# A two-part kernel: the weights and the first image chunk of part two load into two tiles of part one

## The chip, the cores and the metric

The kernel runs on one core of a Trainium2 chip. TensorE (PE) multiplies matrices into PSUM, VectorE (DVE), ScalarE (ACT) and GpSimd (POOL) work on SBUF, and SyncE (SP) issues most of the DMAs; POOL issues the others. The metric is the time of one execution on the device in microseconds, as the median of several runs. One more execution is recorded by the hardware profiler; the profile and the trace are of that one.

## The reference

The input is x, 16 images of 64 channels of 128 x 128, float32. Two layers follow each other.

```
# layer 0: filtered nonlinearity
q = quantile(x over the pixels, 0.5)                # one median per image and channel
x = x + relu(-q)
y = upsample by 2, 7-tap filter along both axes; relu; 7-tap filter; every second pixel
# layer 1: frequency gate, then attention with reduced keys
spec = rfft2(y); gate = sigmoid(w2 gelu(w1 |spec|))
xf   = y + irfft2(spec * gate)
q    = xf as tokens @ q_w + q_b                     # 16384 tokens per image, 4 heads of 16
for (stride, weights) in ((8, sr1), (16, sr2)):     # 256 and 64 positions
    s = layernorm(conv(xf, weights, stride) + b); k, v = s @ kv_w + kv_b; v = depthwise 3x3 of v
out  = softmax(q k^T / 4) v @ proj_w + proj_b + y
```

## The kernel before

The work is done in two parts, `phase1` (line 262) and `phase2` (line 978). Each opens its own SBUF and PSUM pools, and closes them at its end; the second part's tiles lie where the first part's lay. Between them stand two sets of tensors in DRAM: `zd` (the filtered images y) and `xfd` (the gated images xf).

**The first part** goes over 16 images in groups of four channels, 256 groups in all. `filtered` (558) loads a group into one of four `pad` tiles, adds the image's shift on POOL (from a tile `sb`), and does the filters and the two steps of the transform. `gate` (727) and `inverse` (893) follow for each image, some groups later, and store `xfd`. The shifts come from `medians` (330), which takes two images at once: it loads them whole into two tiles, `xm` (302), 128 partitions by 8192 floats each, and finds the median of each of the 128 rows by counting on ACT and DVE. Its end is a chain over SP: `row<-mean` writes the 128 results to DRAM, and `sb<-row` (537) reads them back onto all partitions. POOL cannot shift the first group of a pair of images before `sb` is there. The last pair of images (14 and 15) is decided when some 30 groups are still to come; after that the tiles `xm` are used no more.

**The second part** goes over 256 periods, 16 for each image, of 1024 pixels. In a period it multiplies for the queries of one such stretch (`queries`, 1317, tokens Q), finds the row maxima of the scores of another (M), the exponents of a third (S and T), and the weighted values (V) and the projection (P) of a fourth. `fetch` (1285) loads the pixels (`xa`, by SP) and reorders them on POOL (`xo`). The maxima go from DVE through a small DMA, `carry` (1379, `q<-nt`), into the queries' tile, and the scores S wait for it. The result leaves on POOL's queue.

Keys and values are made by `keys_values` (1047) for two images at a time. It convolves four image chunks `c`, each 128 x 2 x 16 x 128 floats (2.1 MB), held in turn by two tiles `xp`, with the weights `s1` (stride 8) and `s2` (stride 16); each chunk is loaded in eight pieces from `xfd`. For the first two images this stands ahead of everything else (`spread` is false). For the later pairs its steps are spread over the periods of the pair before: `key` sets their place, and `gate_of` ties a load to the queries of a period.

```
key = (start + CONV[1] * c + k // 3) * 100 + 50 if spread else first + c      # line 1083
deps = [gate_of(start + CONV[1] * c + k // 3)] if spread else []
```

**What sets the order.** Both parts collect `Work` items and hand them to `planned` (158), a list scheduler with estimated durations. For each engine it looks at the first 60 items in order of their keys; items that can start now go by key, and when none of them can start soon, the one that can start first goes. In the second part PE keeps to the order of its keys alone. What the plan returns is issued through `put` (122), which holds each engine to that order. An engine does one thing after the other, so an item that must wait holds up what stands behind it; this includes the DMA issues on SP's and POOL's queues.

The loads of the second part's weights are not in a plan: they stand ahead of it.

```
nc.sync.dma_start(out=w2s, in_=w2)      # line 1019
nc.sync.dma_start(out=s1, in_=sr1)
nc.sync.dma_start(out=s2, in_=sr2)
for vb in vbs:
    nc.sync.dma_start(out=vb, in_=vinit)
```

One detail of `load` in `keys_values` (1075): it takes `y`, `i`, `h`, `c` and `xp` as they are when it is made, but `k` as it is when it runs. By then `k` holds the last value of a later loop, 4, so that for the first two images all 32 pieces are issued by SP, and none by POOL; the trace has them so (xp<-xfd on SP: 32).

Of the kernel before, what the change touches and what calls it, by code (L numbers as in the profile page):

```python
# [8 lines left out]
F32 = mybir.dt.float32  # L9
# [9 lines left out]
B, C, H, W = 16, 64, 128, 128  # L19
NPIX = H * W  # L20
HALF = NPIX // 2
# [45 lines left out]
W2_AT, W2_N = _cols(_W2)  # L67
# [36 lines left out]
@with_exitstack  # L104
def spectral_gate_attention(ctx: ExitStack, tc: tile.TileContext, x, cst, vinit, w1, w2, sr1, sr2, out):
    nc = tc.nc

    const = ctx.enter_context(tc.tile_pool(name="const", bufs=1))
    dram = ctx.enter_context(tc.tile_pool(name="dram", bufs=1, space=DRAM))
    csb = const.tile([128, CST_N], F32, name="csb")  # L110
    nc.sync.dma_start(out=csb, in_=cst)

    def cs(name, rows=128):
        return csb[0:rows, CST_AT[name]]

    ident = cs("ident")
    zd = [dram.tile([C, H, W], F32, name=f"zd{b}") for b in range(B)]
    xfd = [dram.tile([C, H, W], F32, name=f"xfd{b}") for b in range(B)]

    last = {}  # L120

    def put(op, *args, **kw):
        engine = op.__self__
        with tc.issue_after(last[engine]) if engine in last else nullcontext():
            out = op(*args, **kw)  # L125
        last[engine] = out.ins
        return out

    phase1(tc, nc, cs, ident, x, w1, dram, zd, xfd, put)
    phase2(tc, nc, cs, ident, vinit, w2, sr1, sr2, zd, xfd, out, put)  # L130


DELAY = {("PE", "ACT"): 267, ("PE", "DVE"): 210}
# [8 lines left out]
class Slot:  # L142


    def __init__(self, kind, fixed=None):
        self.kind, self.fixed, self.users, self.at = kind, fixed, [], None
# [112 lines left out]


@with_exitstack
def phase1(ctx, tc, nc, cs, ident, x, w1, dram, zd, xfd, put):

    G = 4
    NG = C // G
    P = 2 * G
    NP = NG // 2
    wp = ctx.enter_context(tc.tile_pool(name="p1w", bufs=1))
# [12 lines left out]
    sets, rooms = {}, {}  # L281
# [17 lines left out]
    room("pad", 4, G, W + 2 * PAD)  # L299
    room("bank", 2, 512, pool=psp)  # L300
    room("pair", 3, 2, 512, pool=psp)
    xm = [wp.tile([128, HALF], F32, name=f"xm{f}", tag=f"xm{f}") for f in range(2)]
    hit = wp.tile([128, 4096], U8, name="hit", tag="hit")
    hidl = wp.tile([16, 128], F32, name="hidl", tag="hidl")
    for t in sets["pad"]:
# [244 lines left out]
    over = []  # L550
    for b in range(0, B, 2):
        start = (b - 2) * NG
        over = medians(b, over, *((start, start + LAST) if b else (-99, -98)))
# [406 lines left out]
    for b in range(B):  # L960
        gate(b)
        for j in range(NP):
            inverse(b, j)

    for w in planned(works, rooms, AHEAD, STAY, SOON, REST):
        w.run()
# [7 lines left out]
CONV, CHAIN, TAPS = (2, 2), (14, 20, 23, 24, 28), 5  # L974


@with_exitstack
def phase2(ctx, tc, nc, cs, ident, vinit, w2, sr1, sr2, zd, xfd, out, put):

    N = 512  # L980
    NP = HALF // N
# [1 line left out]
    wp = ctx.enter_context(tc.tile_pool(name="p2w", bufs=1))  # L983
    psp = ctx.enter_context(tc.tile_pool(name="p2ps", bufs=1, space=PSUM))

    def tile_(name, *shape, pool=wp):
        return pool.tile(list(shape), F32, name=name, tag=name)

    w2s = tile_("w2s", 128, W2_N)
    s1 = tile_("s1", 128, 4, 8, C)  # L990
    s2 = tile_("s2", 128, 8, 16, C)
    vbs = [tile_(f"vb{i}", 128, 384) for i in range(4)]
    kgs = [tile_(f"kg{i}", 128, 2, NK) for i in range(2)]
    eps = tile_("eps", 128, 1)
    sets, rooms = {}, {}

    def room(kind, n, *shape, pool=wp):
        sets[kind] = [tile_(f"{kind}_{i}", 128, *shape, pool=pool) for i in range(n)]
        rooms[kind] = n
# [9 lines left out]
    room("nm", 4, 32)  # L1009
    room("nt", 4, 32)  # L1010
    room("rd", 2, N // 32)
    room("xp", 2, 2, 16, W)
    room("pair", 4, 2, 512, pool=psp)
    KVN = 2 * NK
    acc, xs, xc, sd = (tile_(n, 128, KVN) for n in ("acc", "xs", "xc", "sd"))
    pads = [tile_(f"vpad{size}", 64, 2, size + 2, size + 2) for size in (16, 8)]
    vt = tile_("vt", 64, 2, NK + NK2)

    nc.sync.dma_start(out=w2s, in_=w2)
    nc.sync.dma_start(out=s1, in_=sr1)  # L1020
    nc.sync.dma_start(out=s2, in_=sr2)
    for vb in vbs:
        nc.sync.dma_start(out=vb, in_=vinit)
    for t in sets["nm"] + pads:
        nc.gpsimd.memset(t, 0.0)
    nc.vector.memset(eps, 1e-5)
# [6 lines left out]
    def tile_of(slot):  # L1033
        return sets[slot.kind][slot.at]
# [3 lines left out]
    def work(engine, took, deps, key, run, every=None, shape=None, takes=(), tiles=range(8), back=False):  # L1038
        w = Work(engine, took, took if every is None else every, deps, key, run, shape, takes, tiles, back)
        works.append(w)  # L1040
        return w
# [3 lines left out]
    known, last_conv, held = {}, [[], []], {}  # L1045

    def keys_values(b, start, spread):
# [3 lines left out]
        first = start * 100  # L1051
        pair_of = {}

        def pe_key(period, k=0):
            return (start + period) * 100 + KV_AT + 0.01 * k if spread else first + period + 0.01 * k
# [9 lines left out]
            return work(engine, took, deps, key, run, back=spread, **kw)  # L1065

        part = {"A": (slice(0, 512), 0, 512), "B": (slice(512, 640), 1, 128)}
        sums = {"A": None, "B": None}
        for c in range(4):
            xp = Slot("xp", c % 2)  # L1070
            loads = []
            for k in range(8):
                y, i, h = k // 4, k // 2 % 2, k % 2

                def load(y=y, i=i, h=h, c=c, xp=xp):
                    src = xfd[b + i].rearrange("c (r d y) w -> y d c r w", y=2, d=4)[y, c]
                    queue = nc.gpsimd if spread or k % 2 else nc.sync
                    put(
                        queue.dma_start, out=tile_of(xp)[64 * y : 64 * y + 64, i, 8 * h : 8 * h + 8],
                        in_=src[:, 8 * h : 8 * h + 8],  # L1080
                    )

                key = (start + CONV[1] * c + k // 3) * 100 + 50 if spread else first + c
                deps = [gate_of(start + CONV[1] * c + k // 3)] if spread else []
                engine = "POOL" if spread or k % 2 else "SP"
                loads.append(
                    work(engine, 3500, deps + loads[:1], key, load, 700 if engine == "POOL" else 60, takes=[] if k else [xp])
                )
            for n, s in enumerate("AB"):
                cols, bank, m = part[s]  # L1090
                ps = Slot("pair", KV_SLOT)
                wgt = s1 if s == "A" else s2

                def convolve(s=s, ps=ps, xp=xp, c=c, bank=bank, m=m, wgt=wgt):
                    o = tile_of(ps)
                    if s == "A":
                        src = tile_of(xp).rearrange("p i a (h f e) -> p (i a) h f e", h=2, f=8)
                        taps = [(wgt[:, c, f, :], src[:, :, :, f, :]) for f in range(8)]
                    else:
                        src = tile_of(xp).rearrange("p i (a s) (f e) -> p (i a) s f e", s=2, f=16)  # L1100
                        taps = [(wgt[:, c + 4 * d, f, :], src[:, :, d, f, :]) for d in range(2) for f in range(16)]
                    for j, (w, x) in enumerate(taps):
                        put(
                            pe.matmul, o[64 * (j % 2) : 64 * (j % 2) + 64, bank, 0:m], w, x,
                            start=(j < 2), stop=(j >= len(taps) - 2),
                        )

                w = work(
                    "PE", 3430, loads, pe_key(CONV[0] + CONV[1] * c + n, n), convolve, shape="128x64", takes=[ps]
                )  # L1110
                xp.users.append(w)

                def add(s=s, ps=ps, c=c, cols=cols, bank=bank, m=m):
                    o = tile_of(ps)[:, bank, 0:m]
                    if c == 0:
                        put(v.tensor_scalar, acc[:, cols], o, wt("srb1" if s == "A" else "srb2", 128), None, ALU.add)
                    elif c < 3:
                        put(v.tensor_tensor, acc[:, cols], o, acc[:, cols], ALU.add)
                    else:
                        n = 2 if s == "A" else 1  # L1120
                        to = xs[:, cols].rearrange("p (a e h) -> p h a e", h=n, e=8)
                        o, a = (t.rearrange("p (a h e) -> p h a e", h=n, e=8) for t in (o, acc[:, cols]))
                        for h in range(n):
                            put(v.tensor_tensor, to[:, h], o[:, h], a[:, h], ALU.add)

                sums[s] = work(
                    "DVE", 760 if m > 128 else 360, [w] + ([sums[s]] if sums[s] else []),
                    pe_key(CONV[0] + CONV[1] * c + n, n) + 1, add,
                )
                ps.users.append(sums[s])  # L1130
# [11 lines left out]
        ps, w = product(CHAIN[0], 1070, list(sums.values()), center, "128x64")  # L1142
# [20 lines left out]
        ps, w = product(CHAIN[1], 1070, squares, spread_, "64x64")  # L1163
# [38 lines left out]
        ps, w = product(CHAIN[2], 1070, normed, keys, "64x128")  # L1202
# [71 lines left out]
    paces = {}  # L1274

    def gate_of(period):
        return paces[period]

    xas, xos, zrs, qs, qe, crossed, es, ex, avs, ons, vdone = {}, {}, {}, {}, {}, {}, {}, {}, {}, {}, {}

# [365 lines left out]
```

## Time and profile before

| | |
|---|---|
| runs | 9550.02 us median of 3 (9549.4 to 9576.27) |
| profiled execution | 9579.59 us, span 9577.8 us |
| mean granted TensorE clock | 0.969 |
| first part, end of its last matmul | 3930.8 us |
| last matmul of the first pair's convolutions | 4017.5 us |
| DMA queue of SP / of POOL | 423.45 MB / 125.88 MB |

All times within the execution count from the start of its span. In a row of the timeline stand the start, the duration, the engine, the line of the kernel, the operation with its output and input tile, and how many of them were merged; in brackets is the idle time of the engine before it and what ended it. Nearly all instructions carry line 125, since `put` issues them, so they are told apart by their tiles. A row of the waits names who waited, for whom, the sum in us, how often, and the longest. A row of the windows gives the length of the stretch, the busy time of PE, PEld, DVE, ACT and POOL with their counts, then the granted TensorE clock, the DMA share and GB/s.

### The profile page before, as it was taken

To read this page: it belongs to the slowest core of one execution; us is meant where nothing else is said; L and a number is where in the kernel's file an instruction comes from. 1 tells how busy PE (TensorE), PEld (TensorE's weight loads), DVE (VectorE), ACT (ScalarE), POOL (GpSimd) and SP (SyncE) were. 2 spreads that over 40 slices of the span, in tenths; PEclk is the share of its full clock that TensorE was granted. 3 is DMA by queue.
4 is the path that set the end of the run, shared out by engine and by line. 5 is a ranking of instruction groups with operands and counts; after the bars stand their busy time and mean duration, and the time that the engine had idled before them with its cause. 6 is when DMAs were issued, how large, how long until landed. Compare 5 with 4: busy or idle time off the path is not lost.

```text
span 9577.8 us, 176847 instructions
## 1 busy us (share of the span) xinstructions
PE 8901.4 (93%) x70144; PEld 4366.4 (46%) x70144; DVE 7588.5 (79%) x11754; ACT 5883.2 (61%) x7833; POOL 1338.7 (14%) x1390
## 2 busy tenths in 40 slices
PE   0798989898989999699999999999999999999999
PEld 0455555555555566344344344344344443444443
DVE  6797878787878787278878878878878778788887
ACT  2869697978787877245545545545555555455555
POOL 0121212121212121011111111111111111111110
PEclk9899999999999999799999999999999999999999
DMA  3132313131313122421121221221211211211111
GB/s 73 45 84 60 96 52 94 53 93 51 95 54 95 52 64 59 99 62 42 45 64 41 52 60 39 55 55 39 62 48 41 63 48 39 71 40 42 39 42 34
DMA packets 603626, 560.76 MB, mean 59 GB/s; under 512 B 86552, under 2 KB 497696, under 8 KB 594336
## 3 DMA queue, kind: packets, MB, share of 16 engines
q1 hardware_dynamic: 560288, 423.45, 16.8%
q0 software_dynamic: 42496, 125.88, 5.3%
q8 instruction: 554, 9.08, 0.4%
q14 instruction: 288, 2.36, 0.1%
HBM read 343.59 MB, written 201.33 MB: 57 GB/s over the span
## 4 chain that ended last, share of the span: by engine, by line
PE 50%; DVE 8%; issue 2%; DMA 2%; ACT 1%; SPq 1%; POOL 0%; ACTq 0%; POOLq 0%; DVEq 0%
PE pair L125 48%; DVE at L125 3%; DVE on L125 2%; DVE nm L125 2%; PE bank L125 2%; DMA q<-nt 1%; SPq L125 1%; DVE rd L125 0%; DMA xp<-xfd 0%; ACT e L125 0%; DVE sd L125 0%; POOL xo L125 0%; DVE vt L125 0%; ACT L125 0%; POOL pad L125 0%
## 5 line engine op out<-in xcount | busy, mean ns | idle before, releaser
L125 ACT ACTIVATE e<-pair 128x1024 f32<-128x1024 f32 x2560 | 2584.5, 1023 | 2566.8 <-PE pair L125 2556.8
L125 DVE TENSOR_REDUCE nm<-pair 128x2 f32<-128x640 f32 x4096 | 3208.6, 818 | 711.0 <-PE pair L125 672.0
L125 PE MATMUL pair<-kg,q 32*128 32x320 f32 x16384 | 2815.5, 468 | 43.9 <-DVE nm L125 41.7
L125 PE MATMUL pair<-q,kg 32*128 32x512 f32 (+1 forms) x12288 | 2644.1, 625 | 33.7 <-DMA q<-nt 28.8
L125 PEld LDWEIGHTS pair<-kg,q 32*128 32x128 f32 x16384 | 1254.7, 185 | 1590.8 <-DVE nm L125 1094.5
L125 DVE SCALAR_TENSOR_TENSOR z<-y,w1s,z 128x512 f32<-128x512 f32 x1536 | 1224.4, 801 | 345.9 <-ACT z L125 322.2
L125 PE MATMUL pair<-e,vb 128*32 128x512 f32 (+1 forms) x12288 | 1273.9, 603 | 0.9 <-DVE ot L125 0.9
L125 DVE SCALAR_TENSOR_TENSOR up<-pad,w1s,up 128x524 f32<-128x524 f32 x1280 | 1041.5, 841 | 181.4 <-ACT up L125 178.9
L125 PEld LDWEIGHTS pair<-q,kg 32*128 32x128 f32 (+1 forms) x12288 | 747.1, 165 | 609.9 <-DVE nm L125 209.2
L125 PE MATMUL pair<-up,w1s 64*128 64x262 f32 x4096 | 657.1, 430 | 312.0 <-DVE up L125 243.6
L125 POOL TENSOR_TENSOR pad<-pad,sb 128x512 f32<-128x512 f32 x256 | 454.9, 1782 | 2449.6 <-DMA pad<-x 1548.5
L125 ACT ACTIVATE r<-pair 128x524 f32<-128x524 f32 x1024 | 576.9, 615 | 153.5 <-PE pair L125 152.7
L125 POOL COPY xo<-xa 128x512 f32<-128x512 f32 x256 | 268.8, 1050 | 2745.2 <-issue 2500.8
L125 PEld LDWEIGHTS pair<-up,w1s 64*128 64x128 f32 x4096 | 400.3, 199 | 518.8 <-DVE up L125 239.6
L125 PE MATMUL pair<-r,w1s 128*64 128x262 f32 x4096 | 580.5, 408 | 44.3 <-ACT r L125 42.4
L125 PEld LDWEIGHTS pair<-e,vb 128*32 128x32 f32 (+1 forms) x12288 | 261.3, 108 | 668.1 <-issue 551.5
L125 POOL DMA_DIRECT2D result<-ot x512 | 272.5, 537 | 2081.9 <-DVE ot L125 2065.0
L125 PE MATMUL pair<-f,csb 128*128 128x260 f32 (+1 forms) x2048 | 521.8, 398 | 17.9 <-ACT f L125 16.4
L125 PE MATMUL bank<-csb,spec 128*64 128x256 f32 x4096 | 502.6, 390 | 15.0 <-ACT rc L125 10.6
L125 ACT ACTIVATE up<-pad,w1s 128x524 f32<-128x524 f32 x512 | 395.2, 805 | 153.3 <-POOL pad L125 153.3
L125 PEld LDWEIGHTS pair<-f,csb 128*128 128x128 f32 x2048 | 374.6, 193 | 157.0 <-issue 49.6
L125 PEld LDWEIGHTS pair<-r,w1s 128*64 128x64 f32 x4096 | 262.6, 140 | 281.6 <-ACT r L125 71.7
(150 smaller groups left out, 9162.3 us busy)
## 6 DMA issues: line engine op xcount, KB each, us to landing
xm<-x SPq DMA_DIRECT2D x128, 512.0 KB
pad<-x SPq DMA_DIRECT2D x256, 256.0 KB
zd<-z SPq DMA_DIRECT2D x256, 256.0 KB
xfd<-xf SPq DMA_DIRECT2D x256, 256.0 KB
xa<-xfd SPq DMA_DIRECT2D x512, 128.0 KB
zr<-zd SPq DMA_DIRECT2D x512, 128.0 KB
result<-ot POOLq DMA_DIRECT2D x512, 128.0 KB, 2.9
xp<-xfd POOLq DMA_DIRECT2D x224, 256.0 KB, 5.3
```

The costliest lines, as they stand in the source:

```text
L125: out = op(*args, **kw)
```

## The change

The two tiles `xm` move into a pool of their own, `kept`, that lasts over both parts. A class `Held` lays tiles of the second part into them: `s1`, `w2s`, the image chunk tile `xp` number 0 and three of the four `vb` into the first, `s2` into the second. `Held.loads` lists 22 loads: the weights `w2s`, three times `vinit`, `s1` in two pieces, `s2` in eight, and chunk 0 of the first two images in eight. The first part makes SP items of them, with keys from group 226 on and dependent on the last medians. The second part loads only the fourth `vb` itself, and for the first two images no chunk 0.

Further, all image loads of the later pairs get keys and gates three periods earlier; loads of chunks 2 and 3 of the first pair depend on the convolutions that free their tile; and `load` now takes `k` as it is when it is made, so that for the first pair every second piece is issued by POOL.

```
+    kept = ctx.enter_context(tc.tile_pool(name="kept", bufs=1))
+    xm = [kept.tile([128, HALF], F32, name=f"xm{f}", tag=f"xm{f}") for f in range(2)]
+    held = Held(xm)
+    phase1(tc, nc, cs, ident, x, w1, dram, zd, xfd, put, xm, held.loads(nc, vinit, w2, sr1, sr2, xfd))
+    phase2(tc, nc, cs, ident, vinit, zd, xfd, out, put, held)
...
+    def loads(self, nc, vinit, w2, sr1, sr2, xfd):
+        yield self.w2s, w2
+        for vb in self.vbs:
+            yield vb, vinit
+        for d in range(0, 4, 2):
+            yield self.s1[:, d : d + 2], sr1[:, d : d + 2]
+        for d in range(8):
+            yield self.s2[:, d], sr2[:, d]
+        for k in range(8):
+            yield image_chunk(self.xp, xfd, 0, 0, k)
...
@@ phase1
-    xm = [wp.tile([128, HALF], F32, name=f"xm{f}", tag=f"xm{f}") for f in range(2)]
...
+    for k, (o, i) in enumerate(late):
+        work("SP", 4000, over, B * NG - 30 + k, lambda o=o, i=i: put(nc.sync.dma_start, out=o, in_=i), 60)
...
@@ phase2
-    w2s = tile_("w2s", 128, W2_N)
-    s1 = tile_("s1", 128, 4, 8, C)
-    s2 = tile_("s2", 128, 8, 16, C)
-    vbs = [tile_(f"vb{i}", 128, 384) for i in range(4)]
+    w2s, s1, s2 = kept.w2s, kept.s1, kept.s2
+    vbs = kept.vbs + [tile_("vb3", 128, 384)]
...
-    room("xp", 2, 2, 16, W)
+    sets["xp"], rooms["xp"] = [kept.xp, tile_("xp1", 128, 2, 16, W)], 2
...
-    nc.sync.dma_start(out=w2s, in_=w2)
-    nc.sync.dma_start(out=s1, in_=sr1)
-    nc.sync.dma_start(out=s2, in_=sr2)
-    for vb in vbs:
-        nc.sync.dma_start(out=vb, in_=vinit)
+    nc.sync.dma_start(out=vbs[3], in_=vinit)
...
@@ keys_values
-            for k in range(8):
-                y, i, h = k // 4, k // 2 % 2, k % 2
-
-                def load(y=y, i=i, h=h, c=c, xp=xp):
+            for k in range(8) if spread or c else ():
+
+                def load(k=k, c=c, xp=xp):
...
-                key = (start + CONV[1] * c + k // 3) * 100 + 50 if spread else first + c
-                deps = [gate_of(start + CONV[1] * c + k // 3)] if spread else []
+                period = start + CONV[1] * c + k // 3 - 3
+                key = period * 100 + 50 if spread else first + c
+                deps = [gate_of(period)] if spread else convs[c - 2] if c > 1 else []
...
     def gate_of(period):
-        return paces[period]
+        return paces[max(0, period)]
```

More of the change, by code (lines that the diff above doesn't have):

```diff
@@ L127, in put, with __init__, image_chunk @@
         return out
-    phase1(tc, nc, cs, ident, x, w1, dram, zd, xfd, put)
-    phase2(tc, nc, cs, ident, vinit, w2, sr1, sr2, zd, xfd, out, put)
+    kept = ctx.enter_context(tc.tile_pool(name="kept", bufs=1))
[3 more added lines that the diff above has]
+    phase2(tc, nc, cs, ident, vinit, zd, xfd, out, put, held)
+class Held:
+    def __init__(self, xm):
+        ends = [0]
+        for n in (4 * 8 * C, W2_N, 2 * 16 * W, 384, 384, 384):
+            ends.append(ends[-1] + n)
+        s1, w2s, xp, *vbs = (xm[0][:, a:b] for a, b in zip(ends, ends[1:]))
+        self.s1, self.w2s, self.vbs = s1.rearrange("p (d f o) -> p d f o", d=4, f=8), w2s, vbs
+        self.xp = xp.rearrange("p (i r w) -> p i r w", i=2, r=16)
+        self.s2 = xm[1].rearrange("p (d f o) -> p d f o", d=8, f=16)
+    def loads(self, nc, vinit, w2, sr1, sr2, xfd):
[8 more added lines that the diff above has]
+            yield image_chunk(self.xp, xfd, 0, 0, k)
+def image_chunk(xp, xfd, b, c, k):
+    y, i, h = k // 4, k // 2 % 2, k % 2
+    rows = xfd[b + i].rearrange("c (r d y) w -> y d c r w", y=2, d=4)[y, c]
+    return xp[64 * y : 64 * y + 64, i, 8 * h : 8 * h + 8], rows[:, 8 * h : 8 * h + 8]
 DELAY = {("PE", "ACT"): 267, ("PE", "DVE"): 210}
@@ L261, in phase1 @@
 @with_exitstack
-def phase1(ctx, tc, nc, cs, ident, x, w1, dram, zd, xfd, put):
+def phase1(ctx, tc, nc, cs, ident, x, w1, dram, zd, xfd, put, xm, late):
     G = 4
@@ L977, in phase2 @@
 @with_exitstack
-def phase2(ctx, tc, nc, cs, ident, vinit, w2, sr1, sr2, zd, xfd, out, put):
+def phase2(ctx, tc, nc, cs, ident, vinit, zd, xfd, out, put, kept):
     N = 512
@@ L1067, in keys_values @@
         part = {"A": (slice(0, 512), 0, 512), "B": (slice(512, 640), 1, 128)}
-        sums = {"A": None, "B": None}
+        sums, convs = {"A": None, "B": None}, []
         for c in range(4):
@@ L1071, in keys_values @@
             loads = []
-            for k in range(8):
-                y, i, h = k // 4, k // 2 % 2, k % 2
-                def load(y=y, i=i, h=h, c=c, xp=xp):
-                    src = xfd[b + i].rearrange("c (r d y) w -> y d c r w", y=2, d=4)[y, c]
+            for k in range(8) if spread or c else ():
+                def load(k=k, c=c, xp=xp):
                     queue = nc.gpsimd if spread or k % 2 else nc.sync
[L1078 to L1081, printed above, removed]
-                key = (start + CONV[1] * c + k // 3) * 100 + 50 if spread else first + c
-                deps = [gate_of(start + CONV[1] * c + k // 3)] if spread else []
+                    o, i = image_chunk(tile_of(xp), xfd, b, c, k)
+                    put(queue.dma_start, out=o, in_=i)
+                period = start + CONV[1] * c + k // 3 - 3
+                key = period * 100 + 50 if spread else first + c
+                deps = [gate_of(period)] if spread else convs[c - 2] if c > 1 else []
                 engine = "POOL" if spread or k % 2 else "SP"
@@ L1088, in keys_values @@
                 )
+            convs.append([])
             for n, s in enumerate("AB"):
@@ L1106, in convolve @@
                         )
+                held = [] if loads or n else [xp]
                 w = work(
-                    "PE", 3430, loads, pe_key(CONV[0] + CONV[1] * c + n, n), convolve, shape="128x64", takes=[ps]
+                    "PE", 3430, loads + convs[c][:1], pe_key(CONV[0] + CONV[1] * c + n, n), convolve, shape="128x64",
+                    takes=[ps] + held,
                 )
                 xp.users.append(w)
+                convs[c].append(w)
                 def add(s=s, ps=ps, c=c, cols=cols, bank=bank, m=m):
```

## The prediction

> **What bounds the kernel now.** I read the engine shares first, then the waits around the seam of the two parts, then what the DMA queue of SP did there, and last two places that the changed issue order touches.
>
> ```profile
> span 9577.8 us, 176847 instructions
> PE 8901.4 (93%) x70144; PEld 4366.4 (46%) x70144; DVE 7588.5 (79%) x11754; ACT 5883.2 (61%) x7833; POOL 1338.7 (14%) x1390
> PE 50%; DVE 8%; issue 2%; DMA 2%; ACT 1%; SPq 1%; POOL 0%; ACTq 0%; POOLq 0%; DVEq 0%
> ```
>
> TensorE is busy for 93% of the span, so only idle TensorE time can be won. The largest single piece is at the seam. In the waits of 3870 to 4200 us:
>
> ```profile
> PE pair L125 <- DMA xp<-xfd: 43.0, 1, 43.0
> DVE eps L1026 <- DMA xfd<-xf: 42.4, 1, 42.4
> ```
>
> The first convolution of the second part (pair<-xp) waits 43.0 us for its image chunk, once. The timeline of SP's queue says why:
>
> ```profile
> 3934.06 0.34 SPq L1019 DMA_DIRECT2D w2s<-w  x1
> 3934.93 0.43 SPq L1021 DMA_DIRECT2D s<-sr  x1
> 3937.52 9.36 SPq L125 DMA_DIRECT2D xp<-xfd  x2
> 3963.06 8.48 SPq L125 DMA_DIRECT2D xp<-xfd  x7
> 3984.21 17.33 SPq L125 DMA_DIRECT2D xp<-xfd  x16
> ```
>
> The reader is to see that nothing of the second part is issued before 3934, that 6 MB of weights stand ahead of the image, and that chunks 2 and 3 (the x16) cannot be issued before the convolutions of chunks 0 and 1 free their tiles. The last convolution's matmul ends at 4017.5 (its row: 3.71 us from 4013.78).
>
> **The change, part by part.** The built order of the instructions is the same in both kernels on PE, DVE and ACT. Only SP and POOL differ, in three places.
>
> *(1) The seam: gain.* After the change chunk 0 and the weights are there. Its convolution starts when ScalarE has emptied the last bank, at 3931.5, and takes the rows at full clock: 3.65 + 0.75 (acc) + 3.71 + 0.35, so it is done at 3940. Chunk 1 goes to a tile of the second part's own pool and still waits for the end of part one: SP issues from 3934.5. With it go vinit (0.20 MB), four xa and two zr loads (0.79 MB) and 2.10 MB of image. At 200 GB/s, about what the queue moved with such loads between 3950 and 4005 (190 to 228), this takes 15.4 us, plus 1.8 until the first packet: it lands at 3951.5. The half of it that POOL now issues stands behind a copy that waits for xa, at about 3940, which fits in that time. Convolution of chunk 1 at half clock, by the rows after such waits (5.78 + 0.75 + 3.71 + 0.35 = 10.6): 3962. Chunk 2 with two more xa: 2.62 MB behind it, 13.1 us: 3964.6, done 3975. Chunk 3 is issued when chunk 1 is done and comes after chunk 2's bytes, 10.5 us more: 3975.1, convolved in 8.2 (4009.28 to 4017.5): end near 3984.5 instead of 4017.5. Gain **33 us**. Bounds: if every chunk is landed and convolved in turn (12.06 us from issue at 3984.21 to landing at 3996.27, plus 10.6) the end is 4007 and the gain 10. If two queues moved 430 GB/s, as the weights did (416 between 3940 and 3950), chunk 1 is there at 3943.5 and the gain is 44. I stay with 200 GB/s, which is the rate of just these loads. What follows (normalising, the tables, the first queries) is as before.
>
> The Trainium skill, page "DMA: Bandwidth & Descriptors", section on the anatomy of a DMA, fits one DMA from GpSimd as 2.0 us plus its bytes at 436 GB/s. By that a chunk of 2.1 MB would take 6.8 us, an estimate from the page; this trace shows 12.06. By the page the gain would be 44 and the whole sum 23 instead of 12.
>
> *(2) The first part: loss.* The 22 added loads carry keys of groups 226 to 247, but the planner lets any work go that can start now, and they can as soon as the last medians are decided. In the built order 18 of them (6.13 MB of weights and tables, 1.05 MB of image) stand in one block behind row<-mean, and one more ahead of sb<-row, the shifts that the last pair of images waits for. In the timelines of SP, POOL and ACT before:
>
> ```profile
> 3426.01 0.34 SPq L125 DMA_DIRECT2D row<-mean  x1
> 3431.91 0.37 SPq L125 DMA_DIRECT2D pad<-x  x1
> 3438.94 0.45 SPq L125 DMA_DIRECT2D sb<-row  x1
> 3442.50 4.49 POOL L125 TENSOR_TENSOR pad<-pad,sb 128x512 f32<-128x512 f32 x4 [7.73 <-DMA sb<-row]
> 3443.66 0.78 ACT L125 ACTIVATE up<-pad,w1s 128x524 f32<-128x524 f32 x1
> ```
>
> POOL already waits 7.73 us for sb, and ACT takes the shifted pad 0.04 us after POOL's first shift can be done (3442.50 + 1.12): there is no slack. In the built program each DMA on this queue waits for the one eight before it. The block's weights need about 15 us (6.13 MB at 416 GB/s), until 3443; sb then waits for the first image load to land, 3445.3, and its own bytes stand behind eight loads and stores of 0.26 MB, 10.5 us at 200 GB/s. So POOL's shift starts at about 3455 instead of 3442.5: 12.7 us. The zd and xfd stores behind the block are as late, in parallel. Queued behind ACT's up are the copies that the inverse transforms need (bt, xf), so PE stops too; it is busy 47.2 of 50 us after that, so nothing gives the time back. Lower bound 6.4 (sb issued at 3445.3 and landing in the 3.56 us of before), upper 15 (with 2 us for PE at half clock after the stop). I take **13**. A gain is excluded: nothing is taken from this stretch.
>
> *(3) The second part: loss.* All later image loads (POOL's) get keys and gates three periods earlier. Their bytes collide with q<-nt, the small transfer that the next scores wait for. SP's xa issues mark the periods:
>
> ```profile
> 4744.21 1.09 SPq L125 DMA_DIRECT2D xa<-xfd  x2
> 4766.02 1.08 SPq L125 DMA_DIRECT2D xa<-xfd  x2
> 4787.56 1.09 SPq L125 DMA_DIRECT2D xa<-xfd  x2
> 4814.22 1.08 SPq L125 DMA_DIRECT2D xa<-xfd  x2
> 4837.87 1.09 SPq L125 DMA_DIRECT2D xa<-xfd  x2
> PE pair L125 <- DMA q<-nt: 4.7, 3, 3.0
> 4800.00:4804.00 4.00, 4.00 (x22) 1.40 (x20) 1.39 (x2) 1.02 (x1) 0.00 (x0) 0.50 0.00 0
> ```
>
> A period without loads takes 20.2 us. With three loads it takes 21.8 and 21.5, with five 26.7, because PE waits 3.0 us and then runs at a granted clock of 0.50. With three loads and a convolution it takes 23.65, no more than 20.2 + 3.65: the convolution covers the transfer. Over the six later pairs of images the excess is 1.3 us per period with three loads and 6.0 per period with five. Before, a pair pays 3, 3 and 5 loads uncovered (8.6 us) and its other loads lie under convolutions. In the built order it now pays 3, 3, 5, 3 and 2 uncovered (10.8, with 0.9 for two); the rest come as 1 + 7 behind a covered period. Six pairs: +13 us. The first such pair now issues 16 loads while the first queries run, ahead of any exponent, and loses its period with five: -6, +1 for the crowding. Sum: loss **8 us**. Bounds: -6 (the added periods cost nothing) and +23 (each at 1.95, the dearest three-load row, in six pairs).
>
> The page "TensorE: Matmul & The Clock Gate", section "What's actually happening", says that the clock falls after an idle window of about 3.4 us. In this trace it fell after 2.95 us of waiting. By the page a five-load period would cost 3 us and not 6, and the first pair would win only 3: the sum would be 9 instead of 12.
>
> *Sum:* 33 - 13 - 8 = 12 us less. The profiled execution took 9579.6 us (1.8 more than its span); it would be 9568. The median of the runs shown is 29.6 us lower; I take the same 12 off it: **9538 us**.
>
> **The rivals.** *A: faster.* sb slips past the block and the earlier loads cost nothing: 33 - 6.4 + 6 = 33 us, 9517. For it: POOL has 86% of its time free. Against it: sb has eight transfers ahead, and at the seam the image stood behind the weights in just that way. It decides where gain minus both losses is over 28.65 us. *B: slower.* The bursts of 1 + 7 loads (before: 1, 2, 3, 2 over two periods) hit q<-nt as five loads do: two bursts in each of seven pairs at 6.0 us are 84 us, 9622. It decides from 2.9 us per burst ((28.65 + 12) / 14). For it: seven loads move 1.84 MB, 9 us. Against: they go out at some 4159 in a period whose next q<-nt is issued at 4171.7, and a convolution follows. *C: the seam gives less.* POOL's half of chunks 1 to 3 stands behind xo copies, so chunks land one after the other: 10 - 13 - 8 = -11, 9561. *D: the loads do not stay "in the last groups"*: that is in the built order already and is term (2).
>
> **How the numbers follow.** Forecast 0.55; A 0.26; B 0.10; C 0.07; 0.02 for what I do not see. 0.3% (28.65 us) is about what a measurement here can tell from no change. Same: 0.55 + 0.07 = 0.62; faster 0.26; slower 0.12. The range: all bounds together give 9506 (44 - 6.4 + 6) to 9578 (10 - 15 - 23); leaving out B and the outer ends of A and C, 9515 to 9562.
>
> **What would show it.** Right: no 43 us wait of PE for xp; convolution 0 at once after part one; chunk 1's convolution some 17 to 20 us after the end of part one; a wait of POOL for sb of about 20 us where there were 7.7, and PE idle for some 12 us near 3446; five periods above 21 us ahead of each later pair's convolutions, one near 26. Wrong: sb landing by 3449; periods with bursts above 24 us; the last of the first convolutions later than 60 us after the end of part one.

## The result

The changed kernel takes 9578.76 us (median), the kernel before, in the runs beside it, 9558.11 us: a ratio of 1.0024, with a 95% interval of 1.0016 to 1.0032. That is some 22 us more (15 to 31), and still inside the 0.3% that I called no change. I had forecast 12 us less, 9538 us with a range of 9515 to 9562; the time lies outside the range and on the other side. Of the 41 us between 9538 and 9578.76, 8 are the kernel before's own: the forecast starts from its first three runs (9550.02), and beside the changed kernel it took 9558.11.

The profiled execution of the changed kernel took 9568.53 us, 10 us under its median; that of the kernel before took 9579.59 us, 21 us over the median that it has here. So the two spans can't be set against each other. A look at the last medians shows where the profiles differ by chance: up to row<-mean both kernels run the same instructions in the same order, and it was issued at 3426.0 us before and at 3406.1 after. That this is chance, and not the tiles' new place, is seen in a later run: `e4_before_shift`, whose first part is that of the kernel before, issued it at 3409.7. From here on I count from row<-mean, and compare stretches and not spans.

The page of the changed kernel, its first lines:

```profile
span 9566.8 us, 176864 instructions
PE 8898.5 (93%) x70144; PEld 4362.6 (46%) x70144; DVE 7585.2 (79%) x11754; ACT 5884.3 (62%) x7833; POOL 1337.5 (14%) x1402
```

The engine shares are the ones of before. The seam did what the change says. In the waits of 3870 to 4200 us the 43.0 us of PE for its first chunk are gone, and this is left (us, how often, longest):

```profile
PE pair L125 <- DMA xp<-xfd: 17.2, 2, 12.3
```

The timeline of PE shows the first convolutions (start, duration, operands, in brackets the wait ahead):

```profile
3933.28 3.99 PE L125 MATMUL pair<-xm 128*64 128x512 f32 x16 [0.73 <-ACT xf L125]
3938.12 4.02 PE L125 MATMUL pair<-xm,xm 128*64 128x128 f32 x64 [0.86 <-DVE acc L125]
3954.45 6.12 PE L125 MATMUL pair<-xp,xm 128*64 128x512 f32 x16 [12.30 <-DMA xp<-xfd]
3966.15 3.97 PE L125 MATMUL pair<-xm 128*64 128x512 f32 x16 [1.08 <-DMA xm<-xfd]
3979.78 5.35 PE L125 MATMUL pair<-xp,xm 128*64 128x512 f32 x16 [4.88 <-DMA xp<-xfd]
3985.98 3.71 PE L125 MATMUL pair<-xp,xm 128*64 128x128 f32 x64 [0.85 <-DVE xs L125]
```

Chunk 0 is convolved at once, and the last convolution is done 57 us after the first part's end, where it was 87. But two lines hold something new: the convolutions that read xm take 3.97 to 3.99 and 4.02 us, where those of before took 3.65 and 3.71.

In the first part the timeline of SP shows the block of added loads, with sb<-row behind it (rows of two stores and of one more added load, between pad<-x and sb<-row, are left out):

```profile
3406.06 0.34 SPq L125 DMA_DIRECT2D row<-mean  x1
3406.45 0.43 SPq L125 DMA_DIRECT2D xm<-w  x1
3406.92 1.38 SPq L125 DMA_DIRECT2D xm<-vinit  x3
3408.34 15.55 SPq L125 DMA_DIRECT2D xm<-sr  x10
3424.84 6.25 SPq L125 DMA_DIRECT2D xm<-xfd  x4
3431.20 3.30 SPq L125 DMA_DIRECT2D pad<-x  x1
3439.34 1.14 SPq L125 DMA_DIRECT2D sb<-row  x1
```

POOL's timeline, its first shift:

```profile
3444.34 5.00 POOL L125 TENSOR_TENSOR pad<-pad,sb 128x512 f32<-128x512 f32 x4 [29.47 <-DMA sb<-row]
```

And PE's timeline behind that:

```profile
3446.69 2.08 PE L125 MATMUL pair<-bt,csb 64*128 64x256 f32 x8 [20.35 <-ACT bt L125]
```

POOL waits 29.5 us for sb where it waited 7.7, and PE stands still for 20.4 us. The shift starts 38.3 us after row<-mean (before: 16.5).

The stretches of the two profiles then give:

| stretch | before | after | difference |
|---|---|---|---|
| row<-mean to the first query (pair<-xo) | 626.4 | 618.6 | -7.8 |
| of it POOL's first shift after row<-mean | 16.5 | 38.3 | +21.8 |
| first query to the last xa load issued | 5379.8 | 5393.7 | +13.9 |
| last xa to the end of the span | 145.6 | 148.4 | +2.8 |

So the seam gained about 29.6 us (7.8 + 21.8), the first part lost 21.8, and there is a loss of 17 us behind it. That makes +9, not +22; which part of the rest is chance, and what the 17 us are, the experiments had to say. My theory was that the burst costs 22 us and the three-period shift 17.

### The profile page after: what moved, and what is told of

Read it like the earlier page. It is cut to its first block, busy times and chain, and to the rows that moved or that the text cites. A ratio compares the mean times of both kernels' runs of the same rounds, so it can differ in the third digit from the quotient of the medians.

```text
span 9566.8 us, 176864 instructions
## 1 busy us (share of the span) xinstructions
PE 8898.5 (93%) x70144; PEld 4362.6 (46%) x70144; DVE 7585.2 (79%) x11754; ACT 5884.3 (62%) x7833; POOL 1337.5 (14%) x1402
## 4 chain that ended last, share of the span: by engine, by line
PE 50%; DVE 8%; issue 3%; DMA 2%; ACT 1%; SPq 1%; POOL 0%; ACTq 0%; DVEq 0%; POOLq 0%
PE pair L125 48%; DVE at L125 3%; DVE on L125 2%; DVE nm L125 2%; PE bank L125 2%; DMA q<-nt 1%; SPq L125 1%; DVE rd L125 0%; ACT e L125 0%; DMA xp<-xfd 0%; POOL xo L125 0%; DVE sd L125 0%; DVE vt L125 0%; ACT L125 0%; DMA xm<-w 0%
## 5 line engine op out<-in xcount | busy, mean ns | idle before, releaser
L125 PE MATMUL pair<-q,kg 32*128 32x512 f32 (+1 forms) x12288 | 2644.7, 626 | 38.1 <-DMA q<-nt 25.2
L125 PE MATMUL pair<-e,xm 128*32 128x512 f32 (+1 forms) x9216 | 951.4, 601 | 0.0
L125 PEld LDWEIGHTS pair<-e,xm 128*32 128x32 f32 (+1 forms) x9216 | 196.2, 108 | 493.0 <-issue 406.8
```

## The experiments

All are timed. Of the first four, three undo or do one thing each, and one (`e3_both`) joins two of them; the times of the kernel before beside them are 9553.99 us for these four, and 9561.11 us for the four after them, so that I compare ratios where the two groups meet.

**The shift undone** (`e1_no_shift`): from the changed kernel,

```
-                period = start + CONV[1] * c + k // 3 - 3
+                period = start + CONV[1] * c + k // 3
```

> The changed kernel with the image loads of the later pairs back in their old periods (the three-period shift undone; everything else of the change stays). It isolates term (3). Theory (from the two traces): the shift costs 17 us, because the loads that lay under convolutions are now 3 and 2 uncovered ones plus bursts of 1 + 7, and each of the four convolution periods is 0.3 us longer; so some 17 us under the changed kernel's 9578.8, 9562, with the periods of a later pair at 21.8, 21.5 and 26.7 and then 23.65 again. The prediction's size would give 8 us, 9571. A rival, that the shift is harmless and the tiles' new place or the first part's burst carries all of the loss: no change, 9579.

Measured: 9567.49 us, ratio to before 1.0013 (1.0003 to 1.0022); the changed kernel has 1.0024. So the shift is worth about 10 us, nearer to the prediction's 8 than to the 17 of my theory. The two intervals overlap, and the profile by itself does not show it: first query to last xa takes 5392.3 us here, 5393.7 in the changed kernel.

**The burst spread** (`e2_spread`):

```
-        work("SP", 4000, over, B * NG - 30 + k, ...)
+        work("SP", 4000, over + [spectra[B * NG - 30 + k]], B * NG - 30 + k, ...)
```

> The changed kernel with its 22 added loads of the first part spread: load k also waits for the spectrum of group 226 + k, so none goes ahead of the last sb<-row. It isolates term (2). Theory (from the two traces): sb<-row is issued 16.5 us after row<-mean again, POOL waits for it 7.7 us and not 29.5, and the first part ends 22 us earlier: 9557 against 9578.8. The prediction's size would give 13 us, 9566. A rival, that the added bytes cost time wherever they stand (8 MB at about 200 GB/s are 40 us of the queue): no gain, and the last 22 groups each some tenths of a us longer.

Measured: 9552.11 us, ratio 0.9999 (0.9990 to 1.0009), some 24 us less than the changed kernel by the ratios. The wait of POOL is as it was before, in its timeline:

```profile
3416.94 4.49 POOL L125 TENSOR_TENSOR pad<-pad,sb 128x512 f32<-128x512 f32 x4 [7.65 <-DMA sb<-row]
```

From row<-mean to the first query this kernel takes 594.9 us, the changed one 618.6. The same bytes, spread over 22 groups, cost nothing that can be seen: from POOL's first shift to the end of part one it takes 485.5 us, before 488.3. So the whole loss came from where they stood.

**Both** (`e3_both`): the two edits together; of the change only the seam and the tiles' place are left.

> Both of the other two edits: loads of the first part spread, image loads of the later pairs in their old periods. What is left of the change is the seam, term (1). Theory (from the two traces): 29 us under the kernel before, 9558.1 - 29 = 9529, and 39 under the changed kernel (22 + 17). The prediction's size of the seam gives 33 under before, 9525. A rival, that something else of the change costs the 13 us that the timed runs show more than the two profiles (22.6 slower against 9): about 9542.

Measured: 9545.41 us, ratio 0.9991 (0.9982 to 1.0000), only 9 us under before, where I had expected 29, and nearest to the rival's "something else". In this profile row<-mean to the first query is 596.8 us, 29.6 less than before: the seam's gain is all there. It is given back later: first query to last xa takes 5388.9 us (before 5379.8: +9.1), and from there to the end 154.2 us (145.6: +8.6). No image load of the later pairs stands elsewhere than before in this kernel. So the tiles themselves, or POOL's pieces, cost up to 18 us somewhere that the prediction had not looked at.

**Only the shift, in the kernel before** (`e4_before_shift`):

```
-                key = (start + CONV[1] * c + k // 3) * 100 + 50 if spread else first + c
-                deps = [gate_of(start + CONV[1] * c + k // 3)] if spread else []
+                period = start + CONV[1] * c + k // 3 - 3
+                key = period * 100 + 50 if spread else first + c
+                deps = [gate_of(period)] if spread else []
...
-        return paces[period]
+        return paces[max(0, period)]
```

> The kernel before with one thing of the change: the later pairs' image loads three periods earlier. Theory: it costs by itself what it costs in the changed kernel, 17 us: 9575 against 9558.1; six pairs at 3, 3, 5, 3, 2 uncovered loads. The prediction's size: 8 us, 9566. A rival, that the shift costs only together with the new seam (chunk 0 of the second pair early, POOL's pieces): no change, 9558.

Measured: 9563.73 us, ratio 1.0011 (1.0002 to 1.0020): some 10 us. First query to last xa takes 5388.7 us, 8.9 more than before. The prediction's size holds, and my 17 falls. Its xa issues mark the periods ahead of a later pair's convolutions:

```profile
4660.16 1.09 SPq L125 DMA_DIRECT2D xa<-xfd  x2
4681.14 1.09 SPq L125 DMA_DIRECT2D xa<-xfd  x2
4702.86 1.08 SPq L125 DMA_DIRECT2D xa<-xfd  x2
4731.16 1.09 SPq L125 DMA_DIRECT2D xa<-xfd  x2
4755.09 1.08 SPq L125 DMA_DIRECT2D xa<-xfd  x2
4775.31 1.09 SPq L125 DMA_DIRECT2D xa<-xfd  x2
```

The reader is to see 21.0, 21.7, 28.3 and 23.9 us, and then 20.2 again. Its convolution periods are 23.65 and 23.71 us, as before. In all four kernels with the kept tiles so far, shifted or not, every second pair of them is 23.97 and 24.00. I had put those 0.3 us down to the bursts of 1 + 7 loads; the kernels without bursts have them too. They belong to the chunks that are read from xm.

**One queue for the first pair's pieces** (`e5_all_sp`), on top of both edits:

```
-                    queue = nc.gpsimd if spread or k % 2 else nc.sync
+                    queue = nc.gpsimd if spread else nc.sync
...
-                engine = "POOL" if spread or k % 2 else "SP"
+                engine = "POOL" if spread else "SP"
```

> The kernel with both edits (loads of the first part spread, image loads in their old periods), and the 24 image pieces of the first pair all issued by SP, none by POOL, as the kernel before has them. Two theories on the 9 us by which the end of the program is longer (last xa to the end of the span 145.6 before, 154.2 with both edits). The first: the added POOL issues cause it, since they move POOL's code so that an instruction fetch falls after the last store; then the end returns to about 146, and the run is some 6 us below the 9545.4 of both edits, less what the seam loses when one queue has all pieces (0 to 10): 9539 to 9549. The second: the tiles kept over both parts cause it; then the end stays at 154. For the seam: if POOL's half stood behind its copies, SP alone is no slower (first query 584 us after sb<-row, as with the split).

Measured: 9544.26 us, ratio 0.9982 (0.9973 to 0.9991), against 0.9991 with both edits alone: the timings don't tell the 9 us from nothing by themselves, but the profile does. Last xa to the end of the span is 145.7 us, as before. And the seam loses nothing: row<-mean to first query 594.0 us, with the split 596.8. So splitting the pieces over two queues won nothing, and the 12 more issues on POOL are what makes the end longer. From the first of the last two stores' issues to the end of the span it takes 5.6 us before, 5.0 with only the shift, 5.6 with all pieces on SP and 7.0 in the kernel with everything together, which has all pieces on SP too; in the six kernels with the 12 issues it takes 11.0 to 12.1.

My theory of why was an instruction fetch behind the last store. The changed kernel has one in its last stretch, 9550 to 9567 (packets, MB, share):

```profile
q0 software_dynamic: 96, 0.26, 7.2%
q14 instruction: 1, 0.01, 0.1%
```

But it ends 9.0 us before the span does, and the kernel with both edits, 9531 to 9548, has none within its span, though its end is as long (12.1 us):

```profile
DMA packets 96, 0.26 MB, mean 15 GB/s; under 512 B 32, under 2 KB 32, under 8 KB 96
q0 software_dynamic: 96, 0.26, 7.2%
```

So the fetch is not what the end waits for. The trace's records of POOL show what is longer: one instruction, DRAIN, behind the last stores. It lasts 4.4 us before and with all pieces on SP, 9.6 in the changed kernel, 10.5 with both edits, and the span ends 0.8 to 1.2 us after it in each. That the 12 issues lengthen it is shown; why they do stays open.

**The chunk on a rounder address** (`e8_aligned`), on top of both edits:

```
-        for n in (4 * 8 * C, W2_N, 2 * 16 * W, 384, 384, 384):
+        for n in (4 * 8 * C, W2_N + 11, 2 * 16 * W, 384, 384, 384):
```

(`w2s` is still the first W2_N = 597 columns.)

> The kernel with both edits, and 11 unused floats behind w2s in the first kept tile, so that the image chunk starts at float 2656 and not 2645 (10624 bytes, a multiple of 64, and not 10580). The convolutions of chunks 0 and 2, which read the chunk in the kept tile, take 3.97 and 4.00 us in all kernels with the change against 3.65 and 3.71 of those that read the other chunk tile. If the odd start of the chunk makes them longer: 3.65 and 3.71 again, 0.31 x 4 x 8 pairs = 10 us less than both edits, 9535. The rival, that reading image and weights out of the same tile (or kept tiles at all) makes them longer: 3.97 and 4.00 stay, 9545.

Measured: 9538.02 us, ratio 0.9978 (0.9969 to 0.9987), 12 us less than both edits by the ratios, where 10 were expected. The groups of PE by shape (count, busy us, mean ns), with both edits:

```profile
L125 PE MATMUL pair<-xm,xm 128*64 128x128 f32 x1024 | 64.0, 282 | 1.6 <-DVE acc L125 1.6
L125 PE MATMUL pair<-xm 128*64 128x512 f32 x256 | 63.8, 639 | 2.7 <-DMA xm<-xfd 2.0 <-ACT xf L125 0.7
```

and with the 11 floats:

```profile
L125 PE MATMUL pair<-xm,xm 128*64 128x128 f32 x1024 | 59.4, 274 | 1.6 <-DVE acc L125 1.6
L125 PE MATMUL pair<-xm 128*64 128x512 f32 x256 | 58.5, 598 | 1.8 <-DMA xm<-xfd 1.1 <-ACT xf L125 0.7
```

Image and weights still come out of the kept tiles, and 598 and 274 ns are what the kernel before has over its later pairs. So it is the address at which the chunk begins, and not the shared tile: 63.8 + 64.0 - 58.5 - 59.4 = 9.9 us. Only these two addresses were tried; which property of them counts is not shown. First query to last xa is 5377.8 us, as good as before.

**The loads under the convolutions** (`e7_covered`): the burst spread, and

```
-                period = start + CONV[1] * c + k // 3 - 3
+                period = start + CONV[1] * c + 1 + k // 4
+                if c == 0:
+                    period = start - 23 + k // 4 if start else 0
```

> The changed kernel with the first part's loads spread, and the later pairs' image loads placed under convolutions, four to a period: chunk 0 under the last convolutions of the pair before (its tile is free there), chunks 1 to 3 under those of the chunk ahead. It tests what term (3) rests on, that an image load costs time only in periods without a convolution, through q<-nt. If that holds, the three periods of 21.8, 21.5 and 26.7 fall to 20.2 in six pairs (9.3 us each, 56), and the convolution periods stay within 0.3 of theirs: 9545 - 56 = 9489. A rival, that the loads cost about the same time wherever they stand: no change from the old places, 9545, with the convolution periods longer by some 1.2 us each.

Measured: 9495.09 us, ratio 0.9934 (0.9920 to 0.9947), 54 us less than both edits by the ratios, where 56 were expected. In its timeline of SP the periods ahead of the convolutions of the later pair:

```profile
4693.48 1.08 SPq L125 DMA_DIRECT2D xa<-xfd  x2
4713.72 1.09 SPq L125 DMA_DIRECT2D xa<-xfd  x2
4733.93 1.08 SPq L125 DMA_DIRECT2D xa<-xfd  x2
4754.15 1.08 SPq L125 DMA_DIRECT2D xa<-xfd  x2
4778.13 1.09 SPq L125 DMA_DIRECT2D xa<-xfd  x2
```

20.2 us three times where there were 21.8, 21.5 and 26.7 in the kernel before; the convolution periods, now with four loads each, are as long as with both edits (23.98, 23.99, 23.65, 23.72). So loads that lay under a convolution, four to a period, cost nothing that can be seen.

**Everything together** (`e9_all`): burst spread, loads under the convolutions, the chunk on its rounder address, the first pair's pieces on SP.

> Everything together: loads of the first part spread, loads of the later pairs under convolutions, the chunk aligned, the first pair's pieces all on SP. If the terms add: 9489 - 10 - 3 = 9476 against 9554 before, a ratio of 0.992. If the covered loads give nothing: about 9532.

Measured: 9474.4 us, ratio 0.9914 (0.9900 to 0.9928), about 82 us under the kernel before and 105 under the changed one. The terms add up to what was expected. The end from the last xa is 145.5 us, the convolution periods are 23.65 and 23.71, those ahead of them 20.2.

## Why the prediction was wrong

*The size of the seam (term 1) was right.* Predicted 33 us, measured 29.6. The convolution of chunk 1 began 21.9 us after the end of part one, where the sum had 20.7, so the 200 GB/s of the trace held. Most of the missing 3.4 us are at chunk 3, which came 47.2 us after the end of part one and not 44.3. By the page "DMA: Bandwidth & Descriptors" of the Trainium skill (its anatomy section: 2.0 us plus the bytes at 436 GB/s) the 3.1 MB up to the end of chunk 1 would take 9.1 us, an estimate from the page, and the convolution would have begun some 13 us after the end of part one; the trace decides against it here. The step that POOL's half fits in the time held, but that half was not needed at all: one queue is as fast.

*The first part (term 2) was the right mechanism and the wrong size.* sb did stand behind the block, ACT's up and PE behind sb, and spreading the loads gave it all back. I had 13 us (at most 15); it was 21.8 in the profile and some 24 in the timed runs. The step that failed is the rate: "The block's weights need about 15 us (6.13 MB at 416 GB/s)", by which they are there 17 us after row<-mean. The windows of the changed kernel show what moved (length, busy times, then clock, DMA share and GB/s):

```profile
3406.00:3410.00 4.00, 4.00 (x34) 2.23 (x34) 4.00 (x4) 3.62 (x5) 3.82 (x3) 1.00 1.08 17
3410.00:3414.00 4.00, 3.56 (x34) 2.01 (x32) 3.96 (x4) 4.00 (x7) 3.36 (x3) 1.00 0.75 36
3414.00:3417.00 3.00, 3.00 (x28) 1.95 (x24) 2.92 (x3) 2.67 (x5) 0.87 (x1) 1.00 0.65 47
3417.00:3420.00 3.00, 1.75 (x16) 1.19 (x14) 1.50 (x2) 1.95 (x3) 0.00 (x0) 1.00 0.83 271
3420.00:3424.00 4.00, 4.00 (x30) 2.72 (x27) 0.00 (x0) 3.40 (x5) 0.00 (x0) 1.00 1.03 414
3424.00:3428.00 4.00, 2.34 (x16) 1.02 (x14) 0.00 (x0) 0.00 (x0) 0.00 (x0) 1.00 1.02 411
3428.00:3432.00 4.00, 0.00 (x0) 0.00 (x0) 0.00 (x0) 0.00 (x0) 0.00 (x0) 0.80 1.02 403
```

It ran at 414 GB/s only from its fourteenth us on; in the first 11 us, with w2s and the three vinit at its head, it moved 17 to 47 GB/s while the DMA engines were busy for 65% or more. By these windows 6.1 MB had moved at 3432, 26 us after row<-mean. So sb was issued 33.3 us after row<-mean and not 19.3. Once issued it took 5.0 us to the shift, not the 10 that I gave it behind eight transfers. So the issue came 14 us later than in the sum, and by luck a second error of 5 us hid a part of that: the term is off by 9.

Why the head was so slow stays open. It is the same in the other kernel with the block, `e1_no_shift` (20 and 52 GB/s in the first 8 us). The trace's packets name w2s: its 128 rows of 2388 bytes took 11.2 us there. At the seam of before, with w2s at the head as well, 197 GB/s in the 3 us from 3934 were followed by 429, and the 128 rows took 1.6 us. I had taken a rate from a stretch in which all engines wait, and used it for one in which they work; but working engines do not explain it by themselves. With the burst spread, w2s is loaded alone, issued at 3508.46, and its rows took 1.3 us while PE and DVE were busy throughout:

```profile
3509.50:3511.50 2.00, 2.00 (x14) 1.81 (x13) 2.00 (x4) 0.67 (x2) 0.00 (x0) 1.00 0.81 246
```

At least two things differ from the block's head, and no run has told them apart: POOL was idle here and busy there (3.82 of the first 4 us), and no block of loads was queued behind this one.

*The shift (term 3) was right:* 8 predicted; alone in the kernel before it cost 8.9 us in the profile and 10 in the timed runs, and undone it gave back 10 (from the changed kernel) and 8 (with the burst spread) in the timed runs. The profiles of these last two pairs give 1.4 and 17.6, since the periods with five loads vary so much from one profile to the next. The periods themselves are nearly as forecast: ahead of each of the six later pairs the changed kernel has four above 21 us (forecast: five) where three had cost time before, and the one with five loads takes 25.2 to 26.5. The burst of 1 + 7 loads (rival B) costs nothing: the convolution periods are the same 23.97 and 24.00 with it and without.

*The decisive step is one that I did not take.* Term 1 took the rows of before, "3.65 + 0.75 (acc) + 3.71", for chunk 0 in the kept tile, where they came out as 3.99 and 4.02, then "What follows ... is as before", and there is no price for the place of the tiles or for POOL's twelve more issues. Each lasts for the whole kernel or sits at its very end, and each was costed at nothing without naming what hides it: 9.9 us for 32 convolutions that read a chunk from float 2645 of a tile, and about 5.5 us (11.1 less 5.6) at the last stores.

| term | predicted | measured | by |
|---|---|---|---|
| 1, seam | -33 | -29.6 | both edits |
| 2, block ahead of sb | +13 | +21.8 (timed 21 to 24) | burst spread |
| 3, loads three periods earlier | +8 | +8.9 (timed 8 to 10) | only the shift, shift undone |
| chunk on an odd address | 0 | +9.9 | rounder address |
| end of the program | 0 | +5.5 | all on SP |
| sum | -12 | +16.5 | whole change: +22 (15 to 31) |

The sum of the parts lies inside the interval of the whole, at its lower end; four of the 32 slow convolutions are the first pair's, so that 1.2 of the 9.9 us are in the seam's 29.6 already. No run shows what the 5 to 7 us between sum and whole are. They may be chance: the periods with five loads vary from 25 to 29 us from one profile to the next, six of them in each run, and the two profiles that have the changed kernel's second part differ by 12.8 us from first query to last xa (5393.7 and, with the burst spread, 5406.5).

Of the rivals, none came as I had put it. C (the seam gives only 10) comes nearest in the whole, 11 us slower than before, and has the wrong place: the seam gave its 30 us, and other places took them back. That both edits together are 9 us faster, about what C gave the seam, is luck.

## What to carry to other kernels

When a tile is laid into another, look at the byte on which it begins, and price every later instruction that reads it: a third of a us is nothing at the seam and 10 us over 32 uses. A load that "belongs to the last groups" must have something that holds it there, or a planner that lets go whatever can start may put it ahead of the one small transfer that everyone waits for. And where a resource is short only in some periods, look for those in which it is covered: the same 224 loads cost 54 us less under the convolutions, more than the whole seam was worth.

## What the runs showed of the hardware

- A matmul whose moving data lie in a chunk that begins at byte 10580 of the kept tile took 639 ns on average (512 columns) and 282 (128 columns); with the chunk at byte 10624 of the same tile, 598 and 274. The weights' place made no difference: the other chunk tile with weights in the kept tiles took 3.65 and 3.71 us as before.
- Twelve more DMA issues on POOL, early in the second part, went with a longer end of the program: 11.0 to 12.1 us from the last stores on in six kernels, 5.0 to 7.0 in the four without them. What is longer is a DRAIN on POOL (9.6 against 4.4 us); an instruction fetch is not the cause.
- A load of 128 rows of 2388 bytes took 11.2 us at the head of a block of loads, 1.6 at the seam of before, and 1.3 with the loads spread. The cause is open.
- Seven image loads in a burst (1.84 MB) under a convolution cost nothing, five in a period without one 4.5 to 9 us.
- The added loads of the first part, some 8 MB, cost 21 to 24 us with 7 MB of them in one block, and nothing that can be seen in pieces over 22 groups.
